# Layer 0 to layer 1: where the weights of the later layers are loaded, and where the last eight states are written

## Chip, core and metric

The kernel runs on one core of a Trainium2 chip. The metric is the time of one execution on the device in microseconds (us). Engines: PE (TensorE), DVE (VectorE), ACT (ScalarE), POOL (GpSimd), SP (SyncE, which here only issues transfers). A transfer (DMA) is issued by an engine's queue and runs beside it.

## What is computed

Four graph layers in a row, each `x = layernorm(x + layer(x, adj))`, on x of 64 graphs x 256 nodes x 256 features and adj of 64 x 256 x 256, all in float32.

```python
# layer 0: a recurrence over the 256 nodes, row i uses the rows already replaced
d = adj.sum(-1); norm_adjT = swapaxes(adj, 1, 2) * where(d != 0, 1 / d, 0)[:, :, None]
def step(h, i):
    x_i   = h_e[:, i]
    x_par = einsum('bj,bjd->bd', norm_adjT[:, i], h)
    r, z  = sigmoid(split(x_i @ W_ioux.T + b_ioux + x_par @ W_iouh.T + b_iouh))
    hc    = tanh(x_i @ W_coux.T + b_coux + (x_par * r) @ W_couh.T + b_couh)
    return h.at[:, i].set(z * x_par + (1 - z) * hc)
# layer 1: relu(norm_adj @ (x @ W.T + b)), norm_adj by the square roots of the degrees
# layer 2: one-head attention masked by adj, with Wq, Wk, Wv, Wo and relu
# layer 3: eight-head attention masked by adj > 0, with Wq, Wk, Wv, Wo
```

Layer 0 is a chain of 256 dependent steps for all graphs at once. Layers 1 to 3 treat each graph by itself.

## The kernel before

**Layer 0** (`_recurrence`) holds one node's state of all 64 graphs as a 128 x 128 tile (two halves of the features on top of each other). The main loop runs `n` over the nodes, N = 256. In the order of the program step `n` turns `xp` on PE, forms the gates on PE and ACT, and the new state on DVE (L631); ACT copies the state into a tile `hs` (L633), of which there are seven. `into_ring` (L640) writes `hs` with two DMAs into a ring `Hw` in SBUF, W = 64 nodes deep; it runs only in the second half of each block of U = 8 steps, two states a step. `flush` (L623) copies stretches of the ring to the DRAM tensor `Hd`: at step 24 of each 32 steps, and after the last step for the last 16 nodes.

What a step needs of earlier nodes comes by three sides. Near nodes are pushed by DVE (L615) and POOL (L647, L651). The *late* side multiplies the ring on PE (L506), sends the product to a DRAM tile `Lb` (L486), fetches it as `late_sb` (L492), and POOL adds it (L827). The *early* side reads old states back from `Hd` into tiles `Hs` (8 KB in each partition, four buffers, in the pool `stream`) and is finished long before the last steps. `load_later` puts a load on a list from which the loop issues up to two a step in the first four steps of a block. All these DMAs go by the SP queue, in the order written.

**Between the layers.** When the pools of `_recurrence` are closed, their SBUF is used again by the pools of `_layers`. `_layers` first loads on ACT's queue eight 256 x 256 weights (L26), three bias rows (L34) and six bias columns (L41), and on SP's queue W1. PE transposes W1 (L52), DVE copies it (L53), and the bias `bv3` is multiplied by W3o on PE (L899) and added to `b3_r` on DVE (L900). This stands in small pools of its own (`l_setup`, `l_setup_ps`), closed before the pools of the main part are opened.

**Layers 1 to 3** (`_layers`) go by an order written out by hand (`ROUND`). In one round five graphs are at different places, so that one graph is finished per round. `Graph.load` issues on SP y (from `Hd`, L983), xin (L985) and ad (L987) of the graph two rounds ahead; `residual_0` (L991, POOL) adds xin to y; then come the statistics on DVE (L913), the power on POOL (L917), the scaling on ACT (L925), transposes on PE (L938), and the products of two times two blocks (L948).

The framework puts in waits: an instruction waits for whatever wrote or read its tiles, and a tile on released memory waits for the last users of that memory. The DMAs take eight semaphores in turn, so that a DMA waits for the eighth before it. `_layer_3` is a slow path that is taken only if a flag is set.

Of the kernel before, what the change touches and what calls it, by code (L numbers as in the profile page):

```python
# [9 lines left out]
F32 = mybir.dt.float32  # L10
# [9 lines left out]
P = 128  # L20


def _load_w(nc, pool, w, name):

    t = pool.tile([P, 2, w.shape[1]], F32, name=name)
    nc.scalar.dma_start(t, w.rearrange("(k p) n -> p k n", p=P))  # L26
    return t


def _load_row(nc, pool, b, name):  # L30

    n = b.shape[0]
    t = pool.tile([P, n], F32, name=name)
    nc.scalar.dma_start(t, b.unsqueeze(0).to_broadcast([P, n]))  # L34
    return t


def _load_col(nc, t, b):

    with nc.allow_non_contiguous_dma(reason="bias vector across partitions"):  # L40
        nc.scalar.dma_start(t, b.rearrange("(c p) -> p c", p=P))  # L41
# [26 lines left out]
        nc.sync.dma_start(dst[s:s + 1], part)  # L68


def _recurrence(tc, ident, Hd, x, adj, W_ioux, b_ioux, W_iouh, b_iouh, W_coux, b_coux, W_couh, b_couh):

# [15 lines left out]
    nc = tc.nc  # L90
    B, N, D = x.shape
    T = 32
    NB = N // T
    U = 8
    LAG = U + 1
    W = 2 * T
    GB = 8
# [5 lines left out]
    with ExitStack() as ctx:  # L103
        const = ctx.enter_context(tc.tile_pool(name="r_const", bufs=1))
# [10 lines left out]
        Hw = const.tile([P, HB, D], F32, name="Hw")  # L115
# [8 lines left out]
        with tc.tile_pool(name="r_setup", bufs=1) as tmp, tc.tile_pool(  # L124
            name="r_setup_ps", bufs=2, space=bass.MemoryType.PSUM
# [59 lines left out]
        with tc.tile_pool(name="r_first", bufs=2) as tmp, tc.tile_pool(  # L185
            name="r_first_ps", bufs=4, space=bass.MemoryType.PSUM
# [52 lines left out]
        def load_later(out, in_, rank):  # L239

            begun = []

            def f(n):
                nc.sync.dma_start(out, in_)
                begun.append(n)

            loads.append((rank, f))
            loads.sort(key=lambda e: e[0])
            return begun
# [113 lines left out]
        def early_load(e, got=[]):  # L363

            _, k, lo, hi, t = early.pop(e)
            rows = hi - lo
            if t == 0:
                Es[k, lo] = dram.tile([2, NG, 4, T, P], F32, name=f"Es_{k}_{lo}", bufs=1)
            Hs = stream.tile([P, GB, D], F32, tag="Hs", name=f"Hs_{k}_{lo}_{t}", bufs=4)
            last = [load_later(  # L370
                Hs[0:rows], Hd[lo:hi, t * GB:(t + 1) * GB, :], 1
            )]
            if t % 2 == 0:
                A = stream.tile([P, 2 * GB, T], F32, tag="A", name=f"A_{k}_{lo}_{t}")
                last.append(load_later(
                    A[0:rows],
                    adj[t * GB:(t + 2) * GB, lo:hi, k * T:(k + 1) * T].rearrange("b j i -> j b i"), 1
                ))
                got[:] = [A]
            early_in.append((last, k, lo, hi, t, Hs, *got))  # L380

        def early_ahead(n):
            ready = [e for e, piece in enumerate(early) if piece[0] <= n]
            if len(early_in) < 4 and ready:

                half = [e for e in ready if early[e][4] % 2 and early[e - 1:e] != [
                    early[e][0:4] + (early[e][4] - 1,)
                ]]
                early_load((half + ready)[0])
# [229 lines left out]
        def flush(lo, hi):  # L619

            for lo, hi, at in ring(max(lo, 0), hi):
                for g in range(2):
                    nc.sync.dma_start(  # L623
                        Hd[lo:hi, g * HB:(g + 1) * HB, :],
                        Hw[g * W + at:g * W + at + hi - lo],
                    )
# [10 lines left out]
        def into_ring():  # L637
            n, hs = ring_in.pop(0)
            for o in range(2):
                nc.sync.dma_start(Hw[n % W::W, :, o * P:(o + 1) * P], hs[o * B:(o + 1) * B])  # L640

        def push_far(j, hs, first, count):

# [65 lines left out]
        for now in range(N):  # L709
# [9 lines left out]
            if n:  # L719

                assert all(j == n - 2 for _, j in pushes)
                hs = state(n - 1)
                end = min((n - 1) // U * U + 2 * U, N)
                to = list(range(n + 1, end))
                near = to[:len(to) - min(FAR[p], len(to) - 1)] if to else []
                far = to[len(near):]
                pushes += [(m, n - 1) for m in near]
                pushes.sort()
                if p == 0:

                    behind = [(n - 1, hs, m, 4) for m in range(end, min(end + U, N), 4)]

                if p > 3:
                    for _ in range(min(2, len(ring_in))):
                        into_ring()
            if p == 0 and U < n + U < N:
# [100 lines left out]
                xq[n // U + 2] = load_x(n // U + 2)  # L837
            if i == 24:
                flush(n - 8 - T, n - 8)
            early_ahead(n)  # L840
            if k + 1 < NB:
                if i == 0:
# [9 lines left out]
        state(N - 1)  # L852
        while ring_in:
            into_ring()
        flush(N - T // 2, N)


def _layers(tc, ident, Hd, Yd, x, adj, w1, b1, l2, l3, out):

# [3 lines left out]


    nc = tc.nc
    B, N, D = x.shape
    HEADS = 8
    HD = D // HEADS  # L870
# [3 lines left out]
    with ExitStack() as ctx:  # L874
        const = ctx.enter_context(tc.tile_pool(name="l_const", bufs=1))
        W1T = const.tile([P, 2, D], F32, name="W1T")
        W2 = {n: _load_w(nc, const, l2["W" + n], f"W2{n}") for n in "qkvo"}
        W3 = {n: _load_w(nc, const, l3["W" + n], f"W3{n}") for n in "qkvo"}
        b1_r = _load_row(nc, const, b1, "b1_r")
        b2_r = _load_row(nc, const, l2["bo"], "b2o_r")  # L880
        b3_r = _load_row(nc, const, l3["bo"], "b3o_r")
        cols = const.tile([P, 6, 2], F32, name="b_cols")
        for s, b in enumerate((l2["bq"], l2["bk"], l3["bq"], l3["bk"], l3["bv"], l2["bv"])):
            _load_col(nc, cols[:, s, :], b)
        mhalf = const.tile([P, 2], F32, name="mhalf")
        nc.gpsimd.memset(mhalf, -0.5)
        ones = const.tile([P, HD], F32, name="ones")
        nc.gpsimd.memset(ones, 1.0)
        far = const.tile([P, B, 2], F32, name="far")
        with tc.tile_pool(name="l_setup", bufs=1) as tmp, tc.tile_pool(  # L890
            name="l_setup_ps", bufs=2, space=bass.MemoryType.PSUM
        ) as tps:
            _load_wT(nc, tmp, tps, w1, ident, lambda c: W1T[:, :, c * P:(c + 1) * P], "w1")

            bv = tmp.tile([P, 2, P], F32, name="bv3")
            nc.vector.tensor_copy(bv, cols[:, 4, :].unsqueeze(2).to_broadcast([P, 2, P]))
            pb = tps.tile([P, D], F32, tag="wt", name="bv3_ps")
            for k in range(2):
                nc.tensor.matmul(pb, bv[:, k, :], W3["o"][:, k, :], start=(k == 0), stop=(k == 1))  # L899
            nc.vector.tensor_add(b3_r, b3_r, pb)  # L900

        io = ctx.enter_context(tc.tile_pool(name="l_io", bufs=3))
        work = ctx.enter_context(tc.tile_pool(name="l_work", bufs=2))
        small = ctx.enter_context(tc.tile_pool(name="l_small", bufs=8))
        ps = ctx.enter_context(tc.tile_pool(name="l_ps", bufs=1, space=bass.MemoryType.PSUM))
        ctx.enter_context(tc.manual_schedule())

        def norm_a(y, t):

# [19 lines left out]

        def bank(name, shape=(P, 2, D)):  # L930
            return ps.tile(list(shape), F32, tag="mm", name=name, bufs=4)

        def flipped(src, t):

# [38 lines left out]
        class Graph:  # L973
# [5 lines left out]

            def load(self):  # L980
                b = self.b
                self.y = io.tile([P, 2, D], F32, tag="y", name=f"y_{b}", bufs=7)
                nc.sync.dma_start(self.y, Hd[:, b, :].rearrange("(c p) d -> p c d", p=P))  # L983
                self.xin = io.tile([P, 2, D], F32, tag="xin", name=f"xin_{b}")
                nc.sync.dma_start(self.xin, x[b].rearrange("(c p) d -> p c d", p=P))  # L985
                self.ad = io.tile([P, 2, N], F32, tag="ad", name=f"ad_{b}", bufs=4)
                nc.sync.dma_start(self.ad, adj[b].rearrange("(c p) m -> p c m", p=P))  # L987


            def residual_0(self):  # L990
# [210 lines left out]
        return nc.values_load(found)  # L1201


def _layer_3(tc, ident, Yd, adj, l3, out):

    nc = tc.nc
# [106 lines left out]
@with_exitstack  # L1313
def kernel(ctx: ExitStack, tc: tile.TileContext, ins, out):
    nc = tc.nc
    x, adj = ins["x"], ins["adj"]
    B, N, D = x.shape
    main = ctx.enter_context(tc.tile_pool(name="main", bufs=1))
    dram = ctx.enter_context(tc.tile_pool(name="dram", bufs=1, space=bass.MemoryType.DRAM))
    ident = main.tile([P, P], F32, name="ident")  # L1320
    make_identity(nc, ident)
    Hd = dram.tile([N, B, D], F32, name="Hd")
    _recurrence(
        tc, ident, Hd, x, adj,
        *(ins["L0_gnn_" + n] for n in (
            "W_ioux", "b_ioux", "W_iouh", "b_iouh", "W_coux", "b_coux", "W_couh", "b_couh"
        )),
    )
    l2, l3 = (
        {w + n: ins[f"{l}_gnn_{w}{n}"] for w in "Wb" for n in "vkqo"} for l in ("L2", "L3")  # L1330
    )
    Yd = dram.tile([B, P, 2, D], F32, name="Yd")
    found = _layers(tc, ident, Hd, Yd, x, adj, ins["L1_gnn_W"], ins["L1_gnn_b"], l2, l3, out)
    with tc.If(found > 0):
        _layer_3(tc, ident, Yd, adj, l3, out)

# [35 lines left out]
```

## Time and profile before

| what | value |
|---|---|
| time, median of 3 runs | 3609.26 us (3601.38 to 3611.15) |
| the profiled execution | 3613.04 us, its span 3611.1 us |
| mean granted PE clock | 0.975 |
| PE busy | 3296.8 us (91%) |
| DVE, ACT, POOL busy | 2375.3 us (66%), 1904.6 (53%), 1485.1 (41%) |
| last state copied by ACT (L633) | 1578.1 us from the start |
| first operation of layer 1 (POOL, L991) | 1610.0 us |
| first product of layer 1 (PE, L948) | 1618.2 us |

The profile is of one execution; its times are counted from the start of its span. A share of busy time is a mean over parts with different limits, so the parts are looked at one by one. Lines are given as "L" and the line number in the kernel before. A name such as `Hd<-Hw` is output and input of an instruction. "SPq" and "ACTq" are the queues by which these engines issue DMAs.

### The profile page before, as it was taken

To read this page: it belongs to the slowest core of one execution; us is meant where nothing else is said; L and a number is where in the kernel's file an instruction comes from. 1 tells how busy PE (TensorE), PEld (TensorE's weight loads), DVE (VectorE), ACT (ScalarE), POOL (GpSimd) and SP (SyncE) were. 2 spreads that over 40 slices of the span, in tenths; PEclk is the share of its full clock that TensorE was granted. 3 is DMA by queue.
4 is the path that set the end of the run, shared out by engine and by line. 5 is a ranking of instruction groups with operands and counts; after the bars stand their busy time and mean duration, and the time that the engine had idled before them with its cause. 6 is when DMAs were issued, how large, how long until landed. Compare 5 with 4: busy or idle time off the path is not lost.

```text
span 3611.1 us, 81391 instructions
## 1 busy us (share of the span) xinstructions
PE 3296.8 (91%) x30374; PEld 2341.3 (65%) x30374; DVE 2375.3 (66%) x7052; ACT 1904.6 (53%) x5026; POOL 1485.1 (41%) x1669
## 2 busy tenths in 40 slices
PE   5599989999889898858999999999999999999998
PEld 4355555555555555536777777777777777777776
DVE  2366767776667777735676666677776667777775
ACT  0145545554445454425666666666666666666664
POOL 2266667766566778722222222222222222222221
PEclk9799999999999999978999999999999999999999
DMA  8746666788876564140111111111111111111100
GB/s 284 215 134 145 157 167 151 165 191 204 193 190 156 156 152 115 57 114 18 45 45 45 45 45 45 45 45 45 45 45 45 45 45 45 45 44 42 45 27 22
DMA packets 389636, 348.48 MB, mean 97 GB/s; under 512 B 107244, under 2 KB 355192, under 8 KB 384120
## 3 DMA queue, kind: packets, MB, share of 16 engines
q1 hardware_dynamic: 367280, 323.84, 33.7%
q10 hardware_dynamic: 21960, 19.41, 1.6%
q8 instruction: 242, 3.96, 0.5%
q14 instruction: 154, 1.26, 0.1%
HBM read 224.01 MB, written 99.61 MB: 90 GB/s over the span
## 4 chain that ended last, share of the span: by engine, by line
PE 71%; DVE 7%; DMA 7%; POOL 5%; issue 4%; ACT 4%; SPq 2%; ACTq 0%; DVEq 0%; POOLq 0%
PE mm L948 13%; PE o L1151 7%; PE rc L590 4%; PE s L1131 4%; PE rc L582 3%; PE mm_2f L948 3%; PE mm_3v L948 3%; PE mm_3f L948 3%; PE mm_g L948 3%; PE mm_t L948 3%; PE mm_2s L948 3%; PE mm_2v L948 3%; PE mm_2w L948 3%; DVE ACC L615 3%; PE tr_x L938 3%
## 5 line engine op out<-in xcount | busy, mean ns | idle before, releaser
L615 DVE SCALAR_TENSOR_TENSOR ACC<-keep,S,ACC 128x128 f32<-128x128 f32 x1712 | 504.1, 344 | 191.9 <-ACT hs L633 175.6
L917 POOL TENSOR_TENSOR rstd<-rstd,mhalf 128x2 f32<-128x2 f32 x256 | 172.9, 693 | 627.9 <-DVE rstd L916 626.2
L651 POOL TENSOR_TENSOR ACC<-ACC,far 128x384 f32<-128x384 f32 (+1 forms) x313 | 371.5, 1187 | 24.6
L1138 DVE TENSOR_TENSOR p<-s,neg 128x512 f32<-128x512 f32 x512 | 317.4, 681 | 69.0 <-PE s L1131 69.0
L582 PE MATMUL rc<-WxT,xqT 128*64 128x256 f32 x2048 | 328.9, 400 | 7.5 <-issue 2.5
L925 ACT ACTIVATE y<-y,shift,rstd 128x256 f32<-128x256 f32 x512 | 273.4, 598 | 92.4 <-DVE shift L923 53.0
L1043 POOL TENSOR_TENSOR y<-y,g 128x512 f32<-128x512 f32 x64 | 80.8, 1262 | 567.7 <-issue 556.8
L647 POOL TENSOR_TENSOR far<-hs,S 128x384 f32<-128x384 f32 (+1 forms) x313 | 304.2, 972 | 4.7
L1139 ACT ACTIVATE p<-p 128x512 f32<-128x512 f32 x512 | 294.8, 626 | 2.6 <-DVE p L1138 1.6
L913 DVE BATCH_NORM_STATS2 st<-y 128x6 f32<-128x256 f32 x512 | 208.9, 408 | 94.6 <-POOL y L1043 89.8
L755 POOL TENSOR_TENSOR ready<-ACC,dinv 128x128 f32<-128x128 f32 x255 | 101.9, 399 | 399.3 <-DVE ACC L615 380.2
L1166 DVE TENSOR_TENSOR y<-y,mm_3f 128x512 f32<-128x512 f32 x64 | 44.0, 687 | 281.3 <-PE mm_3f L948 281.3
L1157 DVE RECIPROCAL rT<-o 128x256 f32<-128x256 f32 x128 | 224.0, 1750 | 0.3 <-PE o L1151 0.3
L1054 ACT ACTIVATE qk<-mm,b_cols 128x256 f32<-128x256 f32 x256 | 107.2, 469 | 203.7 <-PE mm L948 203.7
L1029 ACT COPY xT<-tr_x 128x512 f32<-128x512 f32 x192 | 112.3, 586 | 183.0 <-PE tr_x L938 183.0
L599 ACT COPY xpT<-xpT_ps 128x128 f32<-128x128 f32 x256 | 68.1, 266 | 263.7 <-PE xpT_ps L597 263.7
L590 PE MATMUL rc<-WhT,xpT 128*64 128x128 f32 x2048 | 170.4, 288 | 28.7 <-ACT xpT L599 28.5
L590 PEld LDWEIGHTS rc<-WhT,xpT 128*64 128x64 f32 x2048 | 107.8, 137 | 118.5 <-ACT xpT L599 83.8
L948 PE MATMUL mm<-xT,W2q 128*128 128x256 f32 x512 | 129.4, 396 | 44.6 <-ACT xT L1029 44.6
L582 PE MATMUL z_ps<-WxT,xqT 128*64 128x128 f32 x2048 | 169.8, 287 | 0.0
L1106 ACT ACTIVATE qk<-mm,b_cols 128x256 f32<-128x256 f32 x256 | 107.2, 469 | 118.5 <-PE mm L948 118.5
L1008 POOL TENSOR_TENSOR dis<-dis,mhalf 128x2 f32<-128x2 f32 x64 | 44.1, 689 | 292.0 <-DVE dis L1007 292.0
(167 smaller groups left out, 7988.8 us busy)
## 6 DMA issues: line engine op xcount, KB each, us to landing
xX<-in_x_dram ACTq DMA_DIRECT2D x16, 1024.0 KB
Us<-xu SPq DMA_DIRECT2D x64, 256.0 KB
rows<-in_adj_dram SPq DMA_DIRECT2D x64, 256.0 KB
ACC<-Us SPq DMA_DIRECT2D x32, 512.0 KB
xq<-in_x_dram SPq DMA_DIRECT2D x64, 256.0 KB
Hw<-hs SPq DMA_DIRECT2D x512, 32.0 KB
Es<-eu SPq DMA_DIRECT2D x64, 256.0 KB
early_sb<-Es SPq DMA_DIRECT2D x32, 512.0 KB
```

What stands on the lines that cost most here:

```text
L582: nc.tensor.matmul(G[o * B:(o + 1) * B], xqT[a, i // 2][:, i % 2, kc, h * B:(h + 1) * B], WxT[:, kc, o, gates], start=False, stop=False, s ...
L590: nc.tensor.matmul(G[o * B:(o + 1) * B], hT[:, kc * B:(kc + 1) * B], WhT[:, kc, o, g], start=False, stop=(kc == 1), skip_group_check=True,)
L615: nc.vector.scalar_tensor_tensor(acc[:, 0, :], keep[:, j % 2, :], s, acc[:, 0, :], ALU.mult, ALU.add)
L647: nc.gpsimd.tensor_mul(tmp[:, 0:count, :], hs.unsqueeze(1).to_broadcast(shape), s.unsqueeze(2).to_broadcast(shape),)
L651: nc.gpsimd.tensor_add(acc, acc, tmp[:, 0:count, :])
L913: nc.vector.bn_stats(st, y[:, c, :])
L925: nc.scalar.activation(y[:, c, :], y[:, c, :], AF.Identity, bias=shift[:, c:c + 1], scale=rstd[:, c:c + 1],)
L948: nc.tensor.matmul(pm[:, c, :], lhsT[:, k, c * P:(c + 1) * P], rhs[:, k, :], start=(k == 0), stop=(k == 1),)
L1138: nc.vector.tensor_add(p, s_ps[i], self.neg3)
L1139: nc.scalar.activation(p, p, AF.Exp, scale=ISQ)
L1151: nc.tensor.matmul(o_ps[i * HD:(i + 1) * HD, part, :], ones if part else self.v3_sb[:, k, h * HD:(h + 1) * HD], self.ps_of[hc][i][:, k, :] ...
L1157: nc.vector.reciprocal(rT, o_ps[:, 1, :])
```

## The change

It has four parts.

1. A pool `wide` with four buffers of 8 KB per partition is opened outside of both layers. The early side's `Hs` tiles are taken from it in place of the pool `stream`. At step n = N - 5U (in the counting of the loop, 40 steps before its end) `then` is called: three more tiles of `wide` are taken, and the loads of W1, of the eight weights, three bias rows and six bias columns are put on the list of `load_later`, behind everything else. They go by SP's queue.
2. The last eight states are written from `hs` straight to `Hd`, one state in each step, not into the ring. The eight states before them are flushed from the ring at step N - U + 3; the flush after the loop is gone.
3. In `_layers` W1's transposes and the bias product use the main part's PSUM banks (`bank`) and constant tiles; the pools `l_setup` and `l_setup_ps` are gone.
4. `Graph.load` issues xin, ad, y in place of y, xin, ad.

```diff
@@ _recurrence @@
-            Hs = stream.tile([P, GB, D], F32, tag="Hs", name=f"Hs_{k}_{lo}_{t}", bufs=4)
+            Hs = wide.tile([P, GB, D], F32, tag="wide", name=f"Hs_{k}_{lo}_{t}")
...
             for o in range(2):
-                nc.sync.dma_start(Hw[n % W::W, :, o * P:(o + 1) * P], hs[o * B:(o + 1) * B])
+                to = Hw[n % W::W] if n < N - U else Hd[n]
+                nc.sync.dma_start(to[..., o * P:(o + 1) * P], hs[o * B:(o + 1) * B])
...
-                if p > 3:
+                if p > 3 or n >= N - U:
                     for _ in range(min(2, len(ring_in))):
                         into_ring()
...
+            if n == N - U + 3:
+                assert all(j >= N - U for j, _ in ring_in)
+                flush(N - T // 2, N - U)
+            if n == N - 5 * U:
+                assert not early and not early_in and not loads
+                then(lambda to, of: load_later(to, of, 3))
...
         while ring_in:
             into_ring()
-        flush(N - T // 2, N)
@@ _layers @@
+    nat, W2, W3, b1_r, b2_r, b3_r, cols = weights
...
-        W2 = {n: _load_w(nc, const, l2["W" + n], f"W2{n}") for n in "qkvo"}
-        W3 = {n: _load_w(nc, const, l3["W" + n], f"W3{n}") for n in "qkvo"}
-        b1_r = _load_row(nc, const, b1, "b1_r")
-        b2_r = _load_row(nc, const, l2["bo"], "b2o_r")
-        b3_r = _load_row(nc, const, l3["bo"], "b3o_r")
-        cols = const.tile([P, 6, 2], F32, name="b_cols")
-        for s, b in enumerate((l2["bq"], l2["bk"], l3["bq"], l3["bk"], l3["bv"], l2["bv"])):
-            _load_col(nc, cols[:, s, :], b)
...
-        with tc.tile_pool(name="l_setup", bufs=1) as tmp, tc.tile_pool(
-            name="l_setup_ps", bufs=2, space=bass.MemoryType.PSUM
-        ) as tps:
-            _load_wT(nc, tmp, tps, w1, ident, lambda c: W1T[:, :, c * P:(c + 1) * P], "w1")
...
+        for c in range(2):
+            pt = bank(f"w1_{c}", (P, 2, P))
+            for k in range(2):
+                nc.tensor.transpose(pt[:, k, :], nat[:, c, k * P:(k + 1) * P], ident)
+            nc.vector.tensor_copy(W1T[:, :, c * P:(c + 1) * P], pt)
+
+        nc.vector.tensor_copy(bv, cols[:, 4, :].unsqueeze(2).to_broadcast([P, 2, P]))
+        pb = bank("bv3_ps", (P, D))
+        for k in range(2):
+            nc.tensor.matmul(pb, bv[:, k, :], W3["o"][:, k, :], start=(k == 0), stop=(k == 1))
+        nc.vector.tensor_add(b3_r, b3_r, pb)
+        ctx.enter_context(tc.manual_schedule())
...
             def load(self):
                 b = self.b
-                self.y = io.tile([P, 2, D], F32, tag="y", name=f"y_{b}", bufs=7)
-                nc.sync.dma_start(self.y, Hd[:, b, :].rearrange("(c p) d -> p c d", p=P))
                 self.xin = io.tile([P, 2, D], F32, tag="xin", name=f"xin_{b}")
                 nc.sync.dma_start(self.xin, x[b].rearrange("(c p) d -> p c d", p=P))
                 self.ad = io.tile([P, 2, N], F32, tag="ad", name=f"ad_{b}", bufs=4)
                 nc.sync.dma_start(self.ad, adj[b].rearrange("(c p) m -> p c m", p=P))
+                self.y = io.tile([P, 2, D], F32, tag="y", name=f"y_{b}", bufs=7)
+                nc.sync.dma_start(self.y, Hd[:, b, :].rearrange("(c p) d -> p c d", p=P))
@@ new @@
+def _load_layers(nc, wide, load, w1, b1, l2, l3):
+    t1, t2, t3 = (wide.tile([P, 8, 256], F32, tag="wide", name=f"weights_{l}") for l in (1, 2, 3))
+    nat = t1[:, 0:2]
+    load(nat, w1.rearrange("(c p) d -> p c d", p=P))
...
+    return nat, *W, *rows, cols
```

## The prediction

> **What bounds the kernel now.** I read four views, from coarse to fine: the page's busy and clock rows, the busy time by stretch, the chain of waits, and the timeline of the DMA queue. The clock row has its dip at the turn from layer 0 to layer 1, after the start-up slices (each slice is 90 us):
>
> ```profile
> PE   5599989999889898858999999999999999999998
> PEclk9799999999999999978999999999999999999999
> ```
>
> Before the dip the recurrence is a dependent chain (256 steps, 4.87 us each at the end, from the timeline: transposes at 1558.67, 1563.55, 1568.42). After it PE is busy nine tenths or more and sets the pace. So time lost between them is on no other engine's account: a start that comes d us earlier ends d us earlier, unless the later part has another limit. The stretches around the turn:
>
> ```profile
> 1560.00:1578.00 18.00, 13.38 (x151) 8.53 (x147) 7.51 (x24) 7.09 (x30) 3.30 (x7) 1.00 0.06 16
> 1578.00:1590.00 12.00, 0.00 (x0) 0.00 (x0) 0.00 (x0) 0.14 (x1) 0.00 (x0) 0.58 0.73 93
> 1590.00:1600.00 10.00, 1.09 (x4) 0.72 (x4) 0.80 (x2) 0.00 (x0) 0.16 (x2) 0.50 0.69 225
> 1600.00:1606.00 6.00, 1.86 (x4) 1.17 (x4) 0.29 (x1) 0.00 (x0) 0.00 (x0) 0.50 0.40 84
> 1618.00:1622.00 4.00, 3.76 (x8) 2.50 (x8) 0.43 (x1) 0.19 (x1) 0.00 (x0) 0.50 0.21 71
> 1622.00:1626.00 4.00, 3.22 (x9) 2.57 (x9) 1.87 (x6) 0.00 (x0) 0.00 (x0) 0.50 0.00 0
> ```
>
> (Columns: stretch, length, busy time of PE, its weight loads, DVE, ACT, POOL with counts, granted clock, DMA share, GB/s.) For 28 us all engines nearly stand still while DMA works. Which transfers stand in the path is told by the chain of waits (start, length, what):
>
> ```profile
> 1577.87 0.27 ACT hs L633
> 1578.16 0.50 SPq L640
> 1578.71 2.61 DMA Hw<-hs
> 1581.33 0.31 SPq L623
> 1581.69 10.36 DMA Hd<-Hw
> 1592.49 0.10 POOL mhalf L886
> ...
> 1595.83 5.81 DMA W3o<-in_L_gnn_Wo_dram
> 1601.66 2.06 DMA b_cols<-in_L_gnn_bv_dram
> 1603.75 0.30 DVE bv L896
> 1604.14 2.06 PE bv_ps L899 x4
> 1606.22 0.38 SPq L983
> 1606.64 3.23 DMA xin<-in_x_dram
> 1610.04 1.27 POOL y L991
> ```
>
> From the copy of the last state (done 1578.14) to the first operation of layer 1 (1610.04) there are 31.9 us: 3.2 us to land the state in the ring, 10.7 us to flush the ring to DRAM, 14.1 us of setup (1592.1 to 1606.2: weights and biases, 17 loads one after the other on ACT's queue, then the bias product), and 3.8 us for the first graph's loads.
>
> **The change part by part.**
>
> *The last eight states go straight to DRAM.* Each step of the last eight issues two writes from hs to Hd where it issued two to Hw, and the final 16-state flush is gone. Its first half (states 240 to 247) is flushed at step 251 instead, beside the recurrence. As built, the SP queue then ends with the two writes of state 255, after which the first layer loads follow. I price it on the old clock: the second write is issued by 1579.22 (end of the ring writes on SP's timeline) and the ring write landed at 1581.27, 2.05 us later. The trace has no write of 64 rows to Hd. The nearest DRAM store, Lb<-lb, was issued by 1395.93 and its reader late_sb<-Lb started at 1398.47, so it landed within 2.5 us. Here the Trainium skill speaks against the change: "DMA: Bandwidth & Descriptors", section "Anatomy of one DMA — SWDGE (gpsimd) path", puts most of a transfer's fixed 2.0 us on the receipt from the target memory and calls HBM the heaviest; its section on latency goes to 2 us for an HBM access at high load. By the SBUF row, y's load issues at 1581.3; by that rule perhaps 2 us later (an estimate). I take the row, because the Lb row bounds the difference to 0.45 us and DMA is nearly idle at this place (share 0.06); the 2 us stay in the range.
>
> *The moved flush.* Two DMAs of 256 KB at step 251 are issued about 1555.6, after state 250's copy. With the 10.36 us of the old, twice as large one they land by 1566. Behind them on SP stand the writes of states 251 to 255; the first that has to wait for the flush's semaphore (eight issues later) is state 254's at about 1573.6, 7 us after. Nothing. Even at twice the duration (1576.3) the last state is not held.
>
> *Setup leaves the gap.* 17 issues leave ACT's queue and one (W1) leaves SP's gap; 18 enter SP between steps 217 and 233, at most two per step. ACT had nothing else to do in the gap, so what counts is the 14.1 us of path. What remains after the recurrence is four transposes (1.09 us, rows of L52), two W1T copies (0.80), the bv copy (0.29), four matmuls (2.06) and one add (0.42). As built, the copy, the bias product and POOL's two memsets still wait on every DMA semaphore, because their new tiles lie on released memory. So they start with the landing at 1581.3: copies to 1582.2, bv 1582.6, product 1584.7, add 1585.1. The first graph's y needs longer (next item), and the first statistic on DVE comes after POOL's 1.27 us, at 1585.9. They lie beside it with 0.8 us to spare; cover gone, they would cost what exceeds it.
>
> *Load order.* xin and ad go ahead of y. As built they wait for nothing late, so they issue at 1579.2 and 1579.7 and only y waits for the last state. Behind y on SP stand the loads of graphs 1 and 2, needed 5.4 us later (POOL's second residual at 1615.48 against 1610.04); they start after y as they did before. y issues 1581.35 to 1581.75. A 256 KB load took 2.8 us from issue end to the waiting PE (nat_w, 1592.52 to 1595.35), xin 2.8 to 2.9. So POOL starts layer 1 at 1581.75 + 2.85 = **1584.6** instead of 1610.04: **25.4 us earlier**. In the steady part y now stands behind ad, whose buffer waits for DVE L1075 of four graphs earlier; there loads issue at 2507.15 to 2508.6 for a residual at 2545.50, 37 us ahead. Nothing.
>
> *The loads inside the recurrence.* The place to look is the late side of the same steps, on the same queue:
>
> ```profile
> 1388.26 1.13 SPq L554 DMA_DIRECT2D xq<-in_x_dram  x2
> 1394.58 1.35 SPq L486 DMA_DIRECT2D Lb<-lb  x2
> 1398.47 0.34 SPq L492 DMA_DIRECT2D late_sb<-Lb  x1
> 1404.80 1.27 POOL L827 TENSOR_TENSOR ACC<-ACC,late_sb 128x512 f32<-128x512 f32 x1
> ```
>
> (Start, duration, queue or engine, line, what.) Six weight loads are put in from ACC's load at 1387.6 to the issue of Lb: 6 x 0.5 = 3 us of issue, where SP stood idle from 1389.4 to 1394.6. late_sb lands about 1398.8 + 2.8 = 1401.6; POOL takes it at 1404.8, 3.2 us of slack. 1.5 MB at the 340 GB/s that the trace reaches after 1612 are 4.5 us, mostly over before Lb is issued. I take 0; the upper bound is 4.5 - 3.2 = 1.3 us in each of two blocks, 2.6 us, and no gain is possible. The six column loads have 4-byte elements but cost 0.4 us of issue and 2.06 us to land, at steps with an idle SP: 0. The Hs tiles moved into the shared pool keep their size and their four buffers: 0.
>
> *The ramp of layer 1.* PE is cold there: an eight-matmul product takes 3.79 us (mm_t at 1618.24) against 1.73 from 1663 on. The Trainium skill, "TensorE: Matmul & The Clock Gate", Part 1, says the clock halves after about 3.4 us of idle window and is full after about 3.4 us of sustained work. A shorter gap might therefore keep PE warm, and four products on the chain would save 4 x 1.9 = 7.6 us more (from the cold and warm rows). The rows say otherwise: PE did 7.0 us of work from 1618 to 1626 and the clock stayed 0.50, and one idle stretch from 1650.7 to 1654 was enough for 0.64 and 0.51 in the next two. After the change PE still has only some 6 us of scattered work (1.09 + 2.06 + 1.09 + 1.40 from the same rows) between 1577 and the first product 8.2 us after POOL's start. I take the same cold ramp, shifted: 0.
>
> **Sum.** 0 + 0 + 0 - 25.4 + 0. Profiled execution: span 3611.1 - 25.4 = 3585.7, with 1.9 us around it 3587.6 (from 3613.04). That execution was slower than all three runs shown; their median 3609.26 gives 3609.26 - 25.4 = **3583.9, said as 3584 us**.
>
> **Rivals.**
> 1. *The gap closes only in part* (10%): DRAM writes land late, small layer setup gets in front of the first statistics, and some late-side steps slip. 2 + 1 + 2.6 us, or up to about 10 together: 3589 to 3594. For it: the all-semaphore waits that remain. Against: each has its slack above.
> 2. *PE stays warm* (5%): 25.4 + 7.6 = 33 us, 3576. For it: the idle gap falls from 31 us to about 7. Against: the clock rows above.
> 3. *The change's loads stall the recurrence more than the gap gave* (2%): the late side's exchange queues behind the weights at steps 217 to 233. Each block would have to be late by 25.4 / 2 + 3.2 = 16 us to reach zero gain; at 20 us per block the time is 3609.3 - 25.4 + 2 x 16.8 = 3617. For it: one queue, in order, with a wait on the eighth transfer before. Against: 1.5 MB would have to take 16 us, 94 GB/s, where 340 were seen.
> 4. *It does not do what it says* (3%): the tile of y or xin falls on released memory whose last user is a long transfer, so that the loads start as late as the old setup's end; gain 3.8 us or less, 3606. Against: as built, y waits only for the writes of Hd.
>
> **Numbers.** The forecast has 80%; its own range is 3578 to 3590 (2.6 us and 2 us of cost, 3 us of gain, and 4 us because three runs of before differ by 9.8). The range for 8 in 10 takes in rival 2 and most of rival 1: 3573 to 3595. Below 0.3% (10.8 us), a measurement of this kernel can't tell a change from none. Faster by more: 0.95 (forecast, rivals 1 and 2), within: 0.03 (rival 4), slower: 0.02 (rival 3).
>
> **What would show it.** In the changed profile: no Hd<-Hw in the chain at the turn; Hd<-hs landing about 2.1 to 2.5 us after its issue, then y<-Hd, then POOL's residual 6.5 us after the last state's copy (31.9 now); the same step time of 4.9 us and no wait on late_sb between 1385 and 1470; clock 0.50 and 3.79 us for the first products. I am wrong if POOL starts more than 9 us after the copy, if a DMA wait shows on POOL's L827 line, or if rounds of layer 1 to 3 (30.4 us apart, 2515.07 to 2545.50) change length.

## The result, and the profile after

The changed kernel takes **3584.25 us** (median of 4 runs, 3579.63 to 3590.99) against 3610.2 us before (4 runs, 3601.38 to 3612.8): a ratio of 0.9935, 95% interval 0.9913 to 0.9957. The forecast was 3584.

The profiled execution happens to be the slowest of the four: 3590.99 us, its span 3589.3, 21.8 us shorter than the span of before. These marks cut both spans: the first and the last state (DVE), the end of ACT's copy of the last state 0.35 us behind it, POOL's first operation of layer 1 (the residual `y`), and the end.

| part | before | after | difference |
|---|---|---|---|
| start to the first state | 161.7 | 162.5 | +0.8 |
| recurrence, first to last state | 1416.1 | 1418.0 | +1.9 |
| gap: end of the last state's copy to POOL's residual | 31.9 | 7.5 | -24.4 |
| layers 1 to 3: residual to the end | 2001.0 | 2001.0 | 0.0 |

In these two profiles the whole gain is in the gap, and nothing of it is lost behind. The page's busy and clock rows of the changed kernel:

```profile
PE   5599999999889998869999999999999999999998
PEclk9799999999989999989999999999999999999999
```

The clock's dip at the turn has shrunk from 7 and 8 in two slices to one 8. The busy time by stretch of the changed kernel (stretch, length, then PE, its weight loads, DVE, ACT, POOL with counts, granted clock, DMA share, GB/s) shows what fills the turn:

```profile
1580.00:1588.00 8.00, 3.82 (x12) 2.31 (x12) 1.80 (x6) 0.27 (x1) 0.00 (x0) 0.60 0.56 165
1588.00:1596.00 8.00, 1.37 (x4) 0.68 (x4) 3.74 (x11) 1.96 (x5) 3.88 (x4) 0.50 0.72 239
1596.00:1600.00 4.00, 3.50 (x8) 2.52 (x8) 0.69 (x1) 0.45 (x1) 0.00 (x0) 0.50 0.26 66
```

The 28 us in which the engines stood still are gone; twelve PE operations lie in the first stretch: the setup's eight (four transposes of W1, four of the bias product) and the transposes of the first graph's adj. The clock is 0.50 in the ramp, as before. The chain of waits of the changed kernel (start, length, what):

```profile
1580.54 0.27 ACT hs L635
...
1580.83 0.45 SPq L643
...
1581.32 1.90 DMA Hd<-hs
...
1583.36 4.79 DMA y<-Hd
...
1588.29 1.27 POOL y L994
```

Where the ring write, the 10.36 us flush, the weights, the bias product and xin stood, two transfers are left: the state's store to DRAM, and the read of `y` out of it. A DMA's time in these chains runs from the start of its issue. The store is quick. The read is long: 4.79 us, where the forecast has 3.25 (0.40 of issue and 2.85 behind it).

### The profile page after: what moved, and what is told of

The parts are those of the page before. It is cut to its first block, busy times and chain, and to the rows that moved or that the text cites. A ratio compares the mean times of both kernels' runs of the same rounds, so it can differ in the third digit from the quotient of the medians.

```text
span 3589.3 us, 81428 instructions
## 1 busy us (share of the span) xinstructions
PE 3302.8 (92%) x30374; PEld 2343.2 (65%) x30374; DVE 2376.4 (66%) x7052; ACT 1905.0 (53%) x5026; POOL 1486.9 (41%) x1669
## 4 chain that ended last, share of the span: by engine, by line
PE 72%; DVE 7%; DMA 6%; POOL 6%; issue 4%; ACT 3%; SPq 2%; ACTq 0%; DVEq 0%; POOLq 0%
PE mm L951 13%; PE o L1154 7%; PE rc L592 4%; PE s L1134 4%; PE rc L584 3%; PE mm_2f L951 3%; PE mm_3v L951 3%; PE mm_3f L951 3%; PE mm_g L951 3%; PE mm_t L951 3%; PE mm_2s L951 3%; PE mm_2v L951 3%; PE late L508 3%; PE mm_2w L951 3%; DVE ACC L617 3%
## 5 line engine op out<-in xcount | busy, mean ns | idle before, releaser
L951 PE MATMUL mm<-xT,weights 128*128 128x256 f32 x2048 | 484.0, 385 | 46.1 <-ACT xT L1032 46.1
L951 PEld LDWEIGHTS mm<-xT,weights 128*128 128x128 f32 x2048 | 386.3, 191 | 112.6 <-ACT xT L1032 62.2
L654 POOL TENSOR_TENSOR ACC<-ACC,far 128x384 f32<-128x384 f32 (+1 forms) x313 | 371.8, 1188 | 24.5
L1057 ACT ACTIVATE qk<-mm,weights 128x256 f32<-128x256 f32 x256 | 107.2, 470 | 202.9 <-PE mm L951 202.9
L1109 ACT ACTIVATE qk<-mm,weights 128x256 f32<-128x256 f32 x256 | 107.3, 470 | 118.2 <-PE mm L951 118.2
```

The lines of the kernel that those rows point to most:

```text
L654: nc.gpsimd.tensor_add(acc, acc, tmp[:, 0:count, :])
L951: nc.tensor.matmul(pm[:, c, :], lhsT[:, k, c * P:(c + 1) * P], rhs[:, k, :], start=(k == 0), stop=(k == 1),)
```

## The experiments

Each ratio is to runs of the kernel before made beside the kernel: their median was 3606.46 us (26 runs) for the changed kernel again, the flush put back, the loads on ACT's queue and `y` first, 3604.75 (10) for the loads put back in `_layers`, the loads doubled, the first graphs' loads and PE kept busy, and 3608.73 (11) for the loads 8 steps later and all three together. In what follows the gap is counted as in the table, and **copy to end** is the gap and the layers together: 2032.9 us before, 2008.5 in the first profile of the changed kernel. It leaves out the recurrence, whose time varies between executions (see the end), so it tells small differences apart that the medians can't. Each is of one profile, though, and the clock in the ramp can move it by 1.2 us without any edit to the layers (see `y` first).

### The changed kernel again

> The changed kernel once more, unaltered, to tell the change from the scatter of single executions. Theory A (the whole gain is the shorter gap): from ACT's copy of the last state to POOL's first residual again 7 to 8 us (31.9 before), from that residual to the end 2001 us as in both profiles, time 22 to 28 us below before. The recurrence, from the first state to the last, was 1416.1 us before and 1418.0 after; if the loads put into it cost time (theory B), it is again near 1418 and the 16 steps from state 208 to 224 take about 88 us as in the first profile; if that was scatter (theory A), these 16 steps come back to about 84 us or the excess shows in other stretches.

Median 3584.01 us (6 runs, 3576.0 to 3591.64), ratio 0.994 (0.9923 to 0.9956). Copy to end is 2008.3 and the gap 7.62, so both repeat to about 0.1 us. The recurrence took 1404.5 us, not 1418.0: of the 15 us between the two profiled executions of this kernel 13.4 lie there, 1.4 ahead of the first state. The first profile had lost 4 us in steps 208 to 224, where the weights are loaded (88.05 against 84.08 before). Here these steps took 83.85, so that loss doesn't come with the loads each time: with single loads at this place they took 83.5 to 85.1 us in five of six profiles, and without any loads 83.4 to 84.9 in three.

### The flush put back, the loads left early

```diff
-                to = Hw[n % W::W] if n < N - U else Hd[n]
-                nc.sync.dma_start(to[..., o * P:(o + 1) * P], hs[o * B:(o + 1) * B])
+                nc.sync.dma_start(Hw[n % W::W, :, o * P:(o + 1) * P], hs[o * B:(o + 1) * B])
-                if p > 3 or n >= N - U:
+                if p > 3:
-            if n == N - U + 3:
-                flush(N - T // 2, N - U)
+        flush(N - T // 2, N)
```

> Only the direct stores are undone: the last eight states go to the ring, and 16 states are flushed after the loop. Theory A: the old 10.4 us of flush and its issue stand in the gap again, so 7.5 + 10.7 = 18.2 us from the last copy to POOL's residual, time 10.7 us above the changed kernel (about 0.3%). Rival (the flush was hidden beside the setup, and the setup's loads were the bound): 9 us or less in the gap, time as the changed kernel.

Median 3596.38 (11 runs), ratio to before 0.9974 (0.9961 to 0.9987). Its chain of waits, from the landing in the ring on:

```profile
1573.01 2.60 DMA Hw<-hs
...
1576.09 10.35 DMA Hd<-Hw
...
1587.47 5.53 DMA y<-Hd
...
1593.13 1.27 POOL y L991
```

The gap is 20.7 us, 13.1 more than with direct stores, and copy to end 2021.4. Ring write and flush are the same 2.60 and 10.35 us as before, now with no setup behind them. The gap is 2.5 us longer than expected, in three pieces. The ring write takes 0.7 us more than the direct store that it replaces. `xin` and `ad` are issued only when the flush has landed (at 1586.52 and 1586.96), which puts `y` 0.95 us later. And the read of `y` takes 0.7 us more than in the changed kernel.

### The loads put back behind the recurrence, the direct stores kept

In a first form the list of loads is issued on ACT's queue after the loop, still by the new code.

```diff
-            if n == N - 5 * U:
-                then(lambda to, of: load_later(to, of, 3))
...
         while ring_in:
             into_ring()
+        then(lambda to, of: nc.scalar.dma_start(to, of))
```

> Only the place of the 18 setup loads is undone: they are issued after the last state, on ACT's queue, into the same tiles. Theory A: ACT needs some 10.5 us for the issues, the last column lands 2 us later, then copy 0.3, product 2.06 and add 0.42 stand before DVE's first statistic: it starts about 15 to 17 us after the last copy against 9.0 in the changed kernel, so 6 to 8 us more time, not the 14.1 us that the setup took before, because it no longer begins after the flush and y's load no longer waits for it. Rival (the 14.1 us come back whole): DVE's first statistic 23 us after the last copy. On the recurrence: if the loads in it cost 4 us at states 208 to 224 (theory B), that stretch goes from 88 back to 84 us here.

Median 3605.09 (12 runs), ratio 0.9994 (0.9983 to 1.0005): by the medians the whole gain is gone (copy to end 2024.9). But this is no clean undoing. The waits of the SP queue in this kernel show the flush of step 251 held (group; total us, count, mean us):

```profile
SPq L625 <- DMA weights<-in_L_gnn_bo_dram: 32.6, 1, 32.6
```

The loads and the flush share the eight semaphores that are taken in turn. By the profile SP's flush waited 32.6 us for a semaphore that ACT's loads had, and the last ten stores of states, queued behind it, were issued only between 1591 and 1601. The gap of 26.9 us is that wait's. So the loads were put where they were before, in `_layers`:

```diff
-                then(lambda to, of: load_later(to, of, 3))
...
+        nat = const.tile([P, 2, D], F32, name="nat")
+        nc.sync.dma_start(nat, w1.rearrange("(c p) d -> p c d", p=P))
+        W2 = {n: _load_w(nc, const, l2["W" + n], f"W2{n}") for n in "qkvo"}
...
+            _load_col(nc, cols[:, s, :], b)
```

> The 18 setup loads stand behind the recurrence again, as before in tiles on released memory, W1 on SP's queue and 17 on ACT's; all else is as in the changed kernel. Theory A: they start when the last stores land (2.4 us after the last copy), take some 10 us to issue on ACT, 2 us to land, and 2.8 us follow until DVE is free: DVE's first statistic 17 to 19 us after the last copy (33.2 before, 8.9 in the changed kernel), so the place of the loads is worth 8 to 10 us and the flush the rest. Rival (the setup's 14.1 us come back whole, or more, because SP's loads wait for semaphores that ACT's loads hold): 22 us or more. Nothing changes in the recurrence: 208 to 224 takes 84 to 85 us.

Median 3587.88 (4 runs), ratio 0.995 (0.9935 to 0.9966), by which it isn't told apart from the changed kernel; copy to end 2017.7, 9.3 us more, is of one profile. Its chain of waits:

```profile
1587.64 7.69 DMA y<-Hd
...
1595.49 1.27 POOL y L1000
...
1602.47 2.07 PE bv_ps L938 x4
...
1606.92 3.79 PE mm_t L957 x8
```

POOL starts only 6.7 us later than in the changed kernel (gap 14.2), since the loads now overlap the stores, and DVE's first statistic comes 15.5 us after the copy, not 17 to 19. `y` is issued 6.4 us after the copy (2.55 in the changed kernel), because SP's loads wait in turn for weight loads of ACT's queue (`xin` 1.2 us for W2v, `y` 1.4 us for W3o), and lands late among them. So sharing the semaphores costs something here too. The rest comes on PE: the bias product waits for the last bias column and stands in the order ahead of `tr_ad`, so the first product comes 25.7 us after the copy (15.7 in the changed kernel). By copy to end, with parts 3 and 4 of the change always in: the moved loads without the direct stores bring 11.5 us (2032.9 to 2021.4), the direct stores without the moved loads 15.2 (2032.9 to 2017.7), both 24.5.

### `y` first again

```diff
+                self.y = io.tile([P, 2, D], F32, tag="y", name=f"y_{b}", bufs=7)
+                nc.sync.dma_start(self.y, Hd[:, b, :].rearrange("(c p) d -> p c d", p=P))
                 self.xin = io.tile([P, 2, D], F32, tag="xin", name=f"xin_{b}")
...
-                self.y = io.tile([P, 2, D], F32, tag="y", name=f"y_{b}", bufs=7)
-                nc.sync.dma_start(self.y, Hd[:, b, :].rearrange("(c p) d -> p c d", p=P))
```

> Only the order of the first loads is undone: y, xin, ad. In the changed kernel y took 4.8 us to land with xin and ad ahead of it, against 2.85 forecast. Theory A1 (xin and ad in flight delay y): y lands some 3 us after its issue and xin 3.2 after its own, so POOL's residual is 6.3 to 6.8 us after the last copy against 7.5, the new order loses 1 us. Theory A2 (a read of rows just stored is slow, or the loads behind y delay it): y again takes 4 to 5 us and POOL starts 7.5 to 8.5 us after the copy. Time the same within what can be measured in both.

Median 3585.32 (6 runs), ratio 0.9938 (0.9921 to 0.9956), not told apart from the changed kernel by the medians. Its chain of waits:

```profile
1573.49 1.90 DMA Hd<-hs
...
1576.12 3.02 DMA xin<-in_x_dram
1579.27 1.27 POOL y L994
...
1591.91 2.01 PE mm_g L951 x8
```

The gap is 6.30 us, where five profiles with the changed order have 7.41 to 7.62. With `y` first, nothing is in flight ahead of it. It landed before `xin`, at most 3.5 us after its issue, though other loads followed it as closely and its rows were stored as late; `xin`, last to land now, takes 3.02. So the new load order, the change's fourth part, loses about 1.2 us. That copy to end is even 3.5 us shorter (2004.9) is in part the clock, and that is luck: it came back during the second product (`mm_g` 2.01 us, 3.80 in the changed kernel). In the kernel with the loads 8 steps later (below), whose layers are the changed kernel's, `mm_g` took 2.01 us as well, with a gap of 7.60 and a copy to end of 2007.2. Compared with that one, `y` first is 2.3 us shorter.

### The first graphs' loads inside the recurrence too

The fourth buffer of `wide`, free at that time, takes x and adj of graphs 0 and 1, and graph 0's degrees and transposed adj are computed before `y` is there.

```diff
+                if b < len(first):
+                    self.xin, self.ad = first[b]
...
+        early = ("degrees_a", "degrees_b", "adT")
+        for name in early:
+            getattr(graphs[0], name)()
...
+    t4 = wide.tile([P, 8, 256], F32, tag="wide", name="first")
+    first = [(t4[:, 4 * b:4 * b + 2], t4[:, 4 * b + 2:4 * b + 4]) for b in range(2)]
```

> xin and ad of the first two graphs are loaded inside the recurrence as well, into the fourth of the wide buffers, so that only y is loaded after the last state; and the degrees and the transpose of the first graph's ad are done ahead of its y. Theory A (y was delayed by xin and ad in flight; the degrees stood on the way to the first product): y lands 2.9 us after its issue, POOL's residual 5.4 to 5.9 us after the last copy (7.6), the first product 12 us after it (15.8); from the last copy to the end 3 to 4 us less than 2008.4. Rival (what is saved ahead of the first product is lost to a wait behind it, since the ramp is set by the second graph): 2007 us or more.

Median 3580.74 (5 runs), ratio 0.9933 (0.992 to 0.9947). The gap is 5.98 us and copy to end 2004.5, as expected; but the first product comes 13.4 us after the copy and not 12, and `mm_g` is warm here too (2.01 us), so against the 2007.2 just named the gain is 2.8 us, not 3.9. In its chain `y` lands in 3.37 us, with nothing ahead of it, and in 2.71 us in the kernel that puts all three together, below. That agrees with `y` first: the forecast's 3.25 us lie between them, and 4.79 is the time behind two others.

### PE kept busy over the gap

`idle(count)` multiplies the identity with a weight, for nobody: 14 products after the bias product, 3 after `tr_ad` and 6 after `tr_x` of graph 0.

```diff
+        def idle(count, name):
+            pw = bank(name)
+            for i in range(count):
+                nc.tensor.matmul(pw[:, i % 2, :], ident, W2["q"][:, i % 2, :], start=True, stop=True)
+        idle(14, "warm_0")
```

> The changed kernel with 23 products added on PE whose results nobody reads, 14 behind the bias product, 3 behind the first transposes of ad, 6 behind those of y, so that PE is busy in the gap. Theory A (PE's granted clock is halved by idling and comes back after 4 to 8 us of work): the first product mm_t takes 1.7 to 2.0 us instead of 3.8 and mm_g too; from POOL's residual to the end 3 to 7 us less than 2001. Rival (the clock needs more than these seconds of work, or comes and goes by itself): mm_t 3.8 us, and the end 0 to 2 us later by the added work.

Median 3578.68 (5 runs, 3570.01 to 3597.43), ratio 0.9943 (0.9924 to 0.9963). Its busy time by stretch, columns as above:

```profile
1562.53:1565.95 3.42, 2.49 (x6) 2.06 (x7) 1.24 (x4) 0.00 (x0) 0.00 (x0) 0.50 0.51 165
1565.95:1569.36 3.41, 3.41 (x9) 2.66 (x9) 0.01 (x1) 0.00 (x0) 0.12 (x1) 0.50 0.93 290
1569.36:1572.77 3.41, 3.41 (x17) 3.00 (x17) 1.27 (x5) 0.00 (x0) 1.85 (x2) 1.00 1.02 336
...
1583.01:1586.43 3.42, 0.21 (x2) 0.00 (x0) 1.24 (x6) 0.65 (x2) 1.92 (x2) 1.00 0.00 0
1586.43:1589.84 3.41, 2.59 (x8) 1.37 (x8) 2.48 (x8) 2.39 (x5) 2.85 (x4) 0.50 0.00 0
```

The clock is full from 1569.36, and `mm_t` and `mm_g` take 1.74 and 2.01 us in place of 3.80 each, 3.9 us less together. Copy to end falls by only 1.9 us, to 2006.5, where 3 to 7 were expected: the added products end 0.6 us late themselves (first product 16.3 us after the copy, not 15.7), and after `mm_g` PE has little to do, the clock falls to 0.50 at 1586.43 and a later product of the ramp (`mm_2f`) takes 3.80 again. Against the 2007.2 of the kernel whose `mm_g` is warm without added products, 0.8 us are left.

### The loads in the recurrence: doubled, and moved

```diff
+                spare = wide.tile([P, 8, 256], F32, tag="wide", name="spare")
...
+                            f(n), nc.sync.dma_start(spare[:, at:at + 2], of)
```

Each load of 256 KB is followed in its slot by a second one.

> Each of the nine weight loads inside the recurrence is followed by a second one of the same 256 KB into a spare tile (2.25 MB more, no use of the data). If these loads hold the recurrence up (theory B; 4 us in the first profile of the changed kernel), states 208 to 240 take 174 us or more against 166.3 to 170.5 so far. If DMA has room there and the 4 us were scatter (theory A), 166 to 169 us; the gap to POOL's residual stays 7.5 us.

One run, 3591.38 us. The timeline of the doubled kernel at POOL (start, duration, engine, line, operation, count, then in brackets idle time before it and what ended it):

```profile
1408.23 1.26 POOL L830 TENSOR_TENSOR ACC<-ACC,late_sb 128x512 f32<-128x512 f32 x1 [6.54 <-DMA late_sb<-Lb]
```

and the same line in the second profile of the changed kernel:

```profile
1392.89 1.27 POOL L830 TENSOR_TENSOR ACC<-ACC,late_sb 128x512 f32<-128x512 f32 x1 [0.38 <-DMA late_sb<-Lb]
```

POOL stood 6.54 us for the late side, and steps 208 to 224 took 90.20 us, 6.4 more than the 83.85 of the second profile with single loads. States 208 to 240 took 172.6 us, between the two forecasts. So the mechanism of the prediction's third rival is real, and it begins with the change's own amount: there, POOL waited 0.38 us. With the same single loads in this block it waited 0.82 us in the kernel with PE kept busy and 2.27 in that with the first graphs' loads, without a longer stretch of steps (84.8 and 84.1 us). The measure is the time from the issue of `late_sb`'s fetch to its use by POOL. Without loads it is 6.3 us; with them it was 3.4 to 3.7 us in five of six profiles, the second of the changed kernel among them (in the first, 5.98). Then the loads were begun 8 steps later, behind the 2 MB flush of step 216 (`N - 4 * U`, nothing else changed):

> One edit against the changed kernel: the loads inside the recurrence begin at step 224 and not 216. Theory A (with the doubled loads POOL waited 6.5 us on late_sb, and in one profile of the changed kernel the single loads left nothing of its slack, because they meet the 2 MB flush of step 216): late_sb is used 6 us or more after its issue in all of the last four blocks, with no wait of POOL on it, states 208 to 240 take 165.7 to 168 us. Rival (the slack is lost to the loads alone, wherever they stand): one of the later blocks shows 3 to 4 us between issue and use instead.

One run, 3588.99 us; issue to use 6.34, 6.35, 6.35 and 6.50 us in the last four blocks, no wait, steps 208 to 224 84.14 us, copy to end 2007.2. This place has the full reserve. A gain in time from it isn't shown: one run can't tell, and the waits at the old place had not lengthened the steps.

### All three together

```diff
-            if n == N - 5 * U:
+            if n == N - 4 * U:
```

and with it the early loads of the first graphs and the idle products, here 9, 2, 6 and 7 of them (the last two after the first `mm_g` and `mm_2w`).

> The parts that helped, together: xin and ad of the first two graphs loaded inside the recurrence and the first degrees done early; 24 products that nobody reads on PE, 9 in the gap, 2 behind the first transposes of y, 6 behind the first mm_g, 7 behind the first mm_2w; and the loads inside the recurrence begin 8 steps later, behind the flush of step 216. Theory A: the single savings of the ramp add (3.9 us from the early loads, 1.9 us from the busy PE, 2 to 4 us more where PE fell cold a second time): 1999 to 2003 us from the last copy to the end, against 2008.4; late_sb is used 6 us or more after its issue. Time 5 to 9 us below the changed kernel, which its scatter hardly lets one see. Rival (the ramp is set by something else than the first graph): 2004 us or more.

Median 3578.76 (6 runs, 3573.09 to 3581.86), ratio 0.992 (0.9906 to 0.9934). Copy to end 2004.9 is no better than the 2004.5 of the first graphs' loads alone, although `mm_2f` now takes 2.01. The gains don't add. What the warm `mm_2f` wins is lost right behind it. The chain of this kernel (first two lines), and of the one with the first graphs' loads alone (last two):

```profile
1623.55 2.01 PE mm_2f L959 x8
1629.21 3.65 PE mm L959 x8
...
1623.60 3.80 PE mm_2f L951 x8
1631.04 1.99 PE mm L951 x8
```

The clock falls at 1629.18, between the two, and the next product is cold in place of `mm_2f`. From the copy to the end of that product it is 57.6 us here and 58.5 there; where the last 0.9 us go was not settled. (The chain also has a stretch of 13.7 us that it calls issue, which means that it names no wait. PE is busy for 12.4 us of it.) The interval overlaps that of the changed kernel (0.9923 to 0.9956), so that it beats the changed kernel is likely and not shown.

## Why the prediction was right

- **What bounds the turn.** Right. The layers took 2001.0 us from POOL's start in both profiles, with rounds 30.4 us apart, so each microsecond of the gap came off the end.
- **The direct stores.** The price taken was safe, in part by luck. From the end of its issue (1581.91) the last store landed after 1.3 us, where the ring's row gave 2.05; from the start of issue, 1.90 against 2.61 (1.89 to 1.91 in seven other profiles). The heavier receipt that the Trainium skill gives to HBM ("DMA: Bandwidth & Descriptors", section "Anatomy of one DMA — SWDGE (gpsimd) path"; these are SP's transfers) is not to be seen at this place. But the ring's row was no measure of a memory. Its write goes to two partitions of the ring, and while it ran about two of the 16 DMA engines were at work (share 0.11, 33 GB/s); in the busiest quarter of a microsecond of a direct store it was some seven (0.45, 121 GB/s):

```profile
1579.25:1581.25 2.00, 0.00 (x0) 0.00 (x0) 0.00 (x0) 0.00 (x0) 0.00 (x0) 0.69 0.11 33
...
1581.90:1582.15 0.25, 0.00 (x0) 0.00 (x0) 0.25 (x2) 0.00 (x0) 0.00 (x0) 0.50 0.45 121
```

  (The first line is the kernel before, the second the changed one.) Putting the flush back cost 13.0 us (2008.4 to 2021.4).
- **The moved flush and the eight states' stores.** Right; the SP queue's timeline at the turn of the changed kernel (start, duration, queue, line, transfer, count) shows them free of it:

```profile
1562.22 19.69 SPq L643 DMA_DIRECT2D Hd<-hs  x10
1582.03 0.53 SPq L986 DMA_DIRECT2D xin<-in_x_dram  x1
1582.60 0.45 SPq L988 DMA_DIRECT2D ad<-in_adj_dram  x1
1583.36 0.37 SPq L990 DMA_DIRECT2D y<-Hd  x1
```

  Ten stores in 19.7 us are the last five states at the pace of the steps; the last one's issue ends at 1581.91, 1.1 us after the copy.
- **Setup leaves the gap.** Right that it hides, not in when it starts. Copy, product and POOL's two memsets were to wait for the landing of the last store; the memsets began at 1579.71, the copy of W1T at 1581.39 and the product at 1582.45, all before the store had landed (1583.2). The add on DVE was over at 1584.95, 4.6 us ahead of DVE's first statistic at 1589.59. That the cover of 0.8 us was too small a number did no harm. Putting the loads back cost 9.3 us by copy to end.
- **Load order.** The term that was mis-sized: y was forecast to land 2.85 us after its issue, by the row of a load that had nothing ahead of it, and POOL started 4.56 us after it (issue ended 1583.73, POOL 1588.29), 1.7 us more; 0.7 us of that came back, since y's issue itself was earlier after the copy than forecast. `xin` and `ad`, put ahead of it, were issued only 1.3 and 0.8 us earlier and were still in flight: PE got `ad` at 1585.69, 2.3 us after `y` was issued.

```profile
1585.69 1.12 PE L941 MATMUL tr_ad<-ident,ad 128*128 128x128 f32 x4 [1.20 <-DMA ad<-in_adj_dram]
```

  The gap was 7.5 us and not 6.5; with `y` first it is 6.3, and the difference of about 1.2 us is this order's price. The forecast had booked it as free.
- **The loads inside the recurrence.** The value taken, 0, was right in time, but the slack of 3.2 us was used up: about 2.7 of the 6.3 us between issue and use were gone, and a wait on `late_sb`, one of the prediction's own signs of being wrong, shows in three of six profiles with the single loads (0.38, 0.82 and 2.27 us, the last above the bound of 1.3). The first profile of the changed kernel shows none, and no wait lengthened the steps. In the one run with twice as much they took 6.4 us more.
- **The ramp.** Right in size, with luck in it: `mm_t` and `mm_g` took 3.80 us each, `mm_t` 8.2 us after POOL's start, but where the loads are 8 steps later `mm_g` took 2.01 with the same layers. The reading that 7.0 us of work leave the clock at 0.50 missed what counts, which is how the work falls into pieces of 3.41 us (last section); the 3.4 us that the prediction cites and sets aside are there, as the length of a piece. The rival's price was too high: where PE was kept warm it brought 1.9 us, not 7.6, since the added products delay the first real one and the clock falls again behind them.
- **Sum.** -24.4 in the gap against -25.4 forecast; the medians differ by 25.95. That the medians agree with the forecast to half a microsecond is partly luck: recurrence and start of the profiled runs differ by 2.7 us, and single runs of one kernel by over 10.

## What to carry to other kernels

Where two parts of a kernel follow each other and the engines stand still between, list every transfer on the chain of waits across the turn and ask of each whether it needs the last result; here, of some twenty-five, only the last state's two stores and the read of `y` do. Of the transfers that do, issue the one that depends on the late result with nothing in front of it: what is put ahead "because it waits for nothing" can still be in flight and make the late one later. When loads are moved into a loop, measure how much of the loop's own slack they use and not only the time, and put them beside no other large transfer.

## What the runs showed of the hardware

- **A read behind two others is much slower than with nothing ahead.** From the start of its issue the same 256 KB read of `y` took 2.71 and 3.37 us with nothing ahead, 4.50 to 5.53 as third in line (six chains), and 7.69 among the weight loads. How they share the way was not taken apart.
- **A store to DRAM needn't be slower than one to SBUF.** From the start of issue 64 rows per DMA landed in DRAM after 1.90 us, in the ring after 2.60. The spread over the DMA engines differs too (shares 0.45 and 0.11), so this says nothing of the memories alone.
- **The clock changes in pieces of 3.41 us.** In each of the twelve profiles the granted clock is 0.50 or 1.00, and from one change to the next it is always a multiple of 3.41 us (in the changed kernel 0.50 from 1581.54 to 1605.43, seven pieces, and 1.00 to 1608.84, one). Between 1500 and 1720 us it rose 36 times over the twelve, always behind a piece in which PE was busy for 2.81 us or more; behind the 109 other pieces at 0.50, with 2.77 us or less, it stayed. It fell only behind pieces with 1.8 us or less, though not behind all of them. So short breaks in the work need not matter, and work that lies across two pieces may count in neither. The changed kernel and the one with the loads 8 steps later have the same layers, but the pieces lie otherwise:

```profile
1598.60:1602.02 3.42, 2.64 (x6) 1.62 (x6) 1.63 (x5) 0.00 (x0) 0.00 (x0) 0.50 0.00 0
1602.02:1605.43 3.41, 3.41 (x11) 2.58 (x9) 0.24 (x2) 0.54 (x2) 0.00 (x0) 0.50 0.00 0
...
1596.82:1600.23 3.41, 2.81 (x7) 1.69 (x5) 0.56 (x1) 0.00 (x0) 0.00 (x0) 0.50 0.00 0
1600.23:1603.64 3.41, 2.43 (x12) 1.94 (x12) 1.31 (x6) 0.84 (x2) 0.22 (x1) 1.00 0.00 0
```

  In the changed kernel (first two lines) `mm_t` and `mm_g` begin at 1596.50 and 1601.07. The piece with the end of the one and the start of the other has 2.64 us of work, the clock stays, and all of `mm_g` is cold. In the other (last two) they begin at 1595.85 and 1600.42; the piece with the most of `mm_t` has 2.8 us, the clock rises at 1600.23, and `mm_g` takes 2.01 us. In the kernel with added products the piece from 1562.53 has 2.49 us and brings nothing, the next is full, and the clock rises at 1569.36.
- **Executions differ in the recurrence more than in the layers.** Over twelve profiles of the kernels before, after and in the experiments, the recurrence took 1401.5 to 1418.6 us, also 1404.5 and 1418.0 for the same program; copy to end repeated within 0.2 us in the two profiles of that program. Two steps in three repeat to 0.02 us over all twelve; the rest scatter. Step 218 of the first profile of the changed kernel took 8.30 us, and PE's timeline shows it standing there for no releaser that the profile knows:

```profile
1385.96 0.27 PE L599 MATMUL xpT_ps<-ident,xp 128*128 128x128 f32 x1 [2.01 <-issue]
```

  What holds PE there was not tried and stays open.
